# A two-layer graph network: routed experts in blocks of two sizes, and the key/value work of layer 1 in finer steps with its variances on ScalarE

## The chip, the core and the metric

The kernel runs on one core of a Trainium2 chip. A core has a matrix engine (TensorE; in the profile PE for its matmuls and PEld for its weight loads), a vector engine (VectorE, DVE), an engine for activation functions (ScalarE, ACT), a general engine that here mostly issues indirect transfers (GpSimd, POOL), an engine that issues plain transfers (SyncE, SP), and 16 DMA engines. Every engine works through its own queue in order, and the engines wait for each other by semaphores. The metric is the device time of one execution in microseconds (us), as the median of several.

## What is computed

The network has 3125 nodes with 256 features and 50000 edges sorted by target. Two layers are applied, each adding a message-passing branch, an attention-like branch and then a mixture of experts to the node features x, with layer norms before them. All arithmetic is float32. The parts that the change touches, in short:

```python
# layer 0, experts: 8 of them, every node goes to its best two
shared = gelu(x @ W1s + b1s) @ W2s + b2s
topw, topi = top_k(softmax(x @ Wr), 2)
routed = sum over the two of  weight_e * (gelu(x @ W1p[e] + b1p[e]) @ W2p[e] + b2p[e])
x = x + shared + routed                      # W1p[e] 256x1024, W2p[e] 1024x256

# layer 1, message passing: 4 heads, softmax over the edges into a node
messages = h_fwd[src] * direction[:, 0:1] + h_rev[src] * direction[:, 1:2]   # 64 wide
scores = leaky_relu(messages . attn[head], 0.2)
out[node, head] = sum of messages * exp(score) / sum of exp(score)

# layer 1, mixing: 8 heads of 64, linear in q
k = (k - mean(k)) / sqrt(var(k) + eps);  v = (v - mean(v)) / sqrt(var(v) + eps)
dots = sum over nodes of k^T v;  out = (q @ dots) / n @ Wout + bout
```

## The kernel before

Nodes are held in 25 tiles of 128. The stages run one after another: layer 0's messages and mixing, its shared and then its routed experts, layer 1's edge loop with the mixing beside it, and layer 1's experts. Two of them matter here.

**Routed experts (`layer0_ffn`).** Each (node, expert) pair gets a slot. The slots of one expert are filled up to a multiple of `BLK` = 256, so that every block of 256 slots belongs to one expert; there are `NBLK` = 32 blocks and 8192 slots whatever the routing gives. The generator `routes()` computes the slot numbers with small VectorE instructions and writes each node's row to its two slots with 50 indirect scatters from GpSimd. It is run in steps: `next(steps)` is called between the matmuls of the shared expert, twice per hidden chunk and per output tile, and after the routes the same chain of steps ranks a second sort's keys (`sort_by_high`), which layer 1's experts need.

For a block, `block_in` reads its expert's number, its rows (264 KB) and the expert's W1 (1 MB) and biases with SyncE; `block_second` loads W2 (1 MB). W1 and W2 have two buffers each. `block_turn` transposes the rows on TensorE (L1132) and works out gates and target rows with nine small VectorE instructions. `block_hidden` does 8 x 2 matmuls with W1 as the stationary operand and the block's 256 slots as the moving one (L1163), with a gelu on ScalarE after each pair (L1165); `block_out` does 8 matmuls per 128 slots with the 256 output columns moving (L1175), scales on VectorE (L1178, tile yo, four buffers) and scatters 128 rows with GpSimd. A float32 matmul shows as two passes in the profile. The order on TensorE is hidden(b), transposes(b+1), out(b-1). Nine steps of the chain follow each block. Once the ranks are done, `next(columns)` issues one of 256 scatters of the second sort (tile sorted) beside each gelu, seven or eight a block. These stages are ordered by the framework's scheduler.

**Edge loop (`layer1_mix`).** 391 columns of 128 edges are taken in 50 groups (`SPANS`: one of 4, then 8 each). GpSimd gathers 136 numbers for each edge, one indirect transfer per column (L71), into four group buffers. TensorE, VectorE and ScalarE are scheduled by hand here (`manual_schedule`): each works in the order of the program text. In round i that is:

- `messages(i)`: L1652 to L1662 on VectorE, ending with the maximum of the scores; TensorE transposes that (L1664);
- `weigh(i-1)`: exponents times messages (L1702, L1703, 2048 elements);
- `maximum(i)`: the running maximum (L1671 to L1673), spread over the partitions by TensorE (L1677);
- `products(i-1)`: 8 matmuls of 260 columns (L1709);
- `add(i-2)`: the block sums (VectorE L1717 and L1718, ScalarE copies L1719 and L1721);
- `ones_of(i)`: the one-hot matrix (L1695);
- `exponents(i)`: ScalarE copies the maximum out of PSUM (L1682, tile top_b), VectorE subtracts it (L1683), ScalarE takes the exponents (L1685, L1687);
- in three rounds of four until round 34, then in every one, one step of the generator `galerkin`, the mixing branch.

A step of `galerkin` handles two node tiles: for the tile before, VectorE reduces the squares to 16 variances (L1797), ScalarE takes the square root (L1801), VectorE inverts and scales (L1803, L1804) and TensorE adds to the dots (L1807); for the tile itself TensorE makes keys and values (two times four matmul passes, L276), ScalarE copies them out (L1817) and squares 1024 elements at once (L1819). After the 25 tiles come the weights' product and the final matmuls and adds (L1823 to L1864).

Of the kernel before, what the change touches and what calls it, by code (L numbers as in the profile page):

```python
# [9 lines left out]
F32 = mybir.dt.float32  # L10
# [4 lines left out]
OP = mybir.AluOpType  # L15
# [20 lines left out]
NBLK = 2 * N // BLK + 8  # L36
SLOTS = NBLK * BLK

# [92 lines left out]
class Kernel:  # L131
# [787 lines left out]
    def layer0_ffn(self, arrive, far, sorting):  # L919
# [3 lines left out]
        with ExitStack() as c:  # L923
# [83 lines left out]
            def routes():  # L1007
# [21 lines left out]
                for e in range(NE):  # L1029
                    nc.vector.tensor_tensor_scan(run[:, e, :], cnt[:, e, :], zero, 0.0, OP.add, OP.add)  # L1030
                nbi = big.tile([P, NE], I32, name="nbi")
                nb = big.tile([P, NE], F32, name="nb")
                yield
                nc.vector.tensor_scalar(nb, run[:, :, NT - 1], float(BLK - 1), None, op0=OP.add)
                yield
                nc.vector.tensor_copy(nbi, nb)
                yield
                nc.vector.tensor_scalar(nbi, nbi, BLK.bit_length() - 1, None, op0=OP.logical_shift_right)
                yield
                nc.vector.tensor_copy(nb, nbi)  # L1040
                end = big.tile([P, NE], F32, name="end")
                yield
                nc.vector.tensor_tensor_scan(end, nb, zero[:, :NE], 0.0, OP.add, OP.add)
                first = big.tile([P, NE], F32, name="first")
                yield
                nc.vector.tensor_sub(first, end, nb)


                nc.vector.tensor_sub(run, run, cnt)
                yield  # L1050
                nc.vector.scalar_tensor_tensor(run, first[:, :, None].to_broadcast([P, NE, NT]), float(BLK), run,
                                               op0=OP.mult, op1=OP.add)
                val = big.tile([P, NT, NE], F32, name="val")
                yield
                nc.vector.scalar_tensor_tensor(val, pre, 1.0, run.rearrange("p e t -> p t e"),
                                               op0=OP.add, op1=OP.add)
                yield
# [8 lines left out]
                for i in range(2):  # L1066
# [15 lines left out]
                nc.gpsimd.iota(which, pattern=[[1, NBLK], [0, NE]], base=0, channel_multiplier=0,  # L1082
                               allow_small_or_imprecise_dtypes=True)
                yield
                nc.vector.tensor_tensor(which, which, first[:1, None, :].to_broadcast([1, NBLK, NE]), OP.is_ge)  # L1085
# [23 lines left out]

            def block_in(b):  # L1110
                e = nc.sync.value_load(exi[0:1, b:b + 1], min_val=0, max_val=NE - 1)
# [4 lines left out]
                nc.sync.dma_start(r, self.slots[b * BLK:(b + 1) * BLK, :].rearrange("(i p) w -> p i w", p=128))  # L1116
# [10 lines left out]
            def block_turn(b, b2, r):  # L1127
                xs = hp.tile([128, 2, BLK], F32, name="xs")
                pt = self.ps_a([128, 2, SB, 128])
                for k in range(2):  # L1130
                    for i in range(SB):
                        nc.tensor.transpose(pt[:, k, i, :], r[:, i, k * 128:(k + 1) * 128], self.ident)  # L1132
                nc.vector.tensor_copy(xs, pt.rearrange("p k i b -> p k (i b)"))  # L1133

                own = hp.tile([128, SB, 4], F32, name="own", bufs=3)
                at, mine = own[:, :, 3], own[:, :, 0:2]
                nc.vector.tensor_scalar(at, base, float(b * BLK), None, op0=OP.add)
                nc.vector.tensor_tensor(mine, r[:, :, D + 2:D + 4],
                                        at[:, :, None].to_broadcast([128, SB, 2]), OP.is_equal)
                gt = hp.tile([128, SB, 2], F32, name="gt")  # L1140
# [3 lines left out]
                to = hp.tile([128, SB, 2], F32, name="to")  # L1144
# [6 lines left out]
                nc.vector.scalar_tensor_tensor(toi, at, 2.0 * NP, own[:, :, 0], op0=OP.add, op1=OP.add)  # L1151
                bg = hp.tile([128, SB, D], F32, name="bg", bufs=3)
                for i in range(SB):
                    nc.scalar.activation(bg[:, i, :], b2, AF.Copy, scale=own[:, i, 2:3])
                return xs, own, toi, bg

            def block_hidden(b, w1, b1, xs):
                few = FC - 1 - b % 2
                h = hp.tile([128, FC, BLK], F32, name="h")
                for f in range(FC):  # L1160
                    ph = self.ps_b([128, BLK])
                    for k in range(2):
                        nc.tensor.matmul(ph, w1[:, k, f * 128:(f + 1) * 128], xs[:, k, :],  # L1163
                                         start=(k == 0), stop=(k == 1))
                    ins = nc.scalar.activation(h[:, f, :], ph, AF.Gelu, bias=b1[:, f:f + 1])  # L1165
                    if ranked and f <= few:
# [4 lines left out]
            def block_out(w2, h, own, to, bg):  # L1171
                for i in range(SB):
# [12 lines left out]
            ins = {b: block_in(b) for b in range(2)}  # L1185
            w2 = {b: block_second(ins[b][0]) for b in range(2)}
            turned = block_turn(0, *ins[0][3:])
            output(*pending)
            todo = None
            for b in range(NBLK):  # L1190
                e, w1, b1, _, _ = ins.pop(b)
                xs, *rest = turned
                h = block_hidden(b, w1, b1, xs)
                if b + 2 < NBLK:
                    ins[b + 2] = block_in(b + 2)
                if b + 1 < NBLK:
                    turned = block_turn(b + 1, *ins[b + 1][3:])
                if todo is not None:
                    block_out(w2.pop(b - 1), *todo)
                    if b + 1 < NBLK:  # L1200
                        w2[b + 1] = block_second(ins[b + 1][0])
                for _ in range(9):
                    ranked = next(steps, sorted_) is sorted_
                todo = h, *rest
            block_out(w2.pop(NBLK - 1), *todo)
# [1434 lines left out]
```

## Time and profile before

| | us |
|---|---|
| three runs | 2496.76, 2501.61, 2501.92; median 2501.61 |
| the profiled execution | 2496.96, span 2495.2 |
| routed experts, first hidden matmul to last output matmul | 941.5 to 1398.1 |
| edge loop, first to last gather | 1463.7 to 1978.1 |
| busy over the span | PE 2052.0, DVE 1465.5, ACT 829.8, POOL 1565.4 |

The profile is taken from one execution on the chip. A group line gives the source line, engine, operation, tiles written and read, shape and count, then the busy time, the mean nanoseconds of one instruction, and the idle time of its engine just before it with what ended that. A timeline line gives the start, the length, engine, line, operation, tiles and shapes; a bracket gives the idle time before it and what released it. A line of a stretch gives each engine's busy time in it, the granted TensorE clock as a share, the busy share of the DMA engines and GB/s.

### The profile page before, as it was taken

How to read it: one execution, taken by the hardware profiler on the slowest of the kernel's cores; microseconds unless marked ns; L12 is line 12 of the kernel's file. 1: busy time of each engine (PE TensorE's matmuls, PEld its weight loads, DVE VectorE, ACT ScalarE, POOL GpSimd, SP SyncE). 2: the span in 40 equal slices, each digit the busy share in tenths (PEclk: the TensorE clock that was granted, in tenths of full speed). 3: DMA queues.
4: the chain of work that ended last, by engine and by line, in shares of the span. 5: the costliest groups of instructions: out<-in, count | busy, mean ns of one | idle time of the engine just before them, and what ended most of it. 6: DMA issues, size and time to landing. Idle time of an engine off the chain costs nothing.

```text
span 2495.2 us, 27313 instructions
## 1 busy us (share of the span) xinstructions
PE 2052.0 (82%) x8239; PEld 1450.5 (58%) x8239; DVE 1465.5 (59%) x3870; ACT 829.8 (33%) x1804; POOL 1565.4 (63%) x1931
## 2 busy tenths in 40 slices
PE   1666799899879989999999647777778779999955
PEld 0433355445555678888888535545556566667644
DVE  6888858986724793221212448888887872223346
ACT  1453144564412113333333324444430042222314
POOL 5888888885000816766666247777776427777743
PEclk9986799999959999999999869999989859999977
DMA  8612539113000225666666332222222112113242
GB/s 269 217 63 102 219 134 324 68 62 111 7 34 5 102 77 164 201 193 200 198 191 187 116 99 55 56 55 56 55 62 46 38 27 38 28 21 80 57 126 78
DMA packets 191721, 263.31 MB, mean 106 GB/s; under 512 B 57234, under 2 KB 152071, under 8 KB 191563
## 3 DMA queue, kind: packets, MB, share of 16 engines
q1 hardware_dynamic: 137551, 211.02, 25.5%
q0 software_dynamic: 48864, 45.64, 8.8%
q10 hardware_dynamic: 5148, 4.80, 0.7%
q8 instruction: 67, 1.10, 0.2%
q14 instruction: 91, 0.75, 0.1%
HBM read 180.80 MB, written 80.55 MB: 105 GB/s over the span
## 4 chain that ended last, share of the span: by engine, by line
PE 59%; DVE 23%; ACT 5%; DMA 4%; POOL 4%; issue 4%; ACTq 0%; DVEq 0%; SPq 0%; POOLq 0%
PE pb L1163 9%; PE pc L1175 8%; PE pb L594 7%; PE fpy L1958 7%; PE fph L1942 7%; DVE v L1703 3%; PE pc L594 3%; PE pw L1709 2%; PE pb L967 2%; PE pc L980 2%; POOL adj L78 2%; PE pb L638 2%; POOL g L71 1%; PE pc L1439 1%; DVE msg L1653 1%
## 5 line engine op out<-in xcount | busy, mean ns | idle before, releaser
L71 POOL DMA_INDIRECT g<-tab,t_src x391 | 378.3, 968 | 197.4 <-issue 153.2
L78 POOL DMA_INDIRECT adj<-ch_sum,ch_place x391 | 415.3, 1062 | 91.0 <-issue 56.5
L78 POOL DMA_INDIRECT sorted<-src,pos x256 | 245.1, 958 | 141.6 <-DVE pos L1462 62.1
L71 POOL DMA_INDIRECT G<-tabg,g_src x256 | 257.9, 1008 | 78.0 <-DMA G<-tabg,g_src 35.7
L1163 PE MATMUL pb<-xs,w 128*128 128x256 f32 x1024 | 226.4, 379 | 0.8 <-ACT h L1165 0.8
L1175 PE MATMUL pc<-w,h 128*128 128x256 f32 x1024 | 226.1, 379 | 0.0
L1709 PE MATMUL pw<-v,hot 128*128 128x260 f32 x782 | 219.5, 442 | 0.0
L1163 PEld LDWEIGHTS pb<-xs,w 128*128 128x128 f32 x1024 | 194.4, 190 | 27.8 <-ACT h L1165 1.0
L594 PE MATMUL pb<-adj,sup 128*128 128x448 f32 (+1 forms) x484 | 196.5, 551 | 14.3 <-DVE r_tot L1309 13.6
L1175 PEld LDWEIGHTS pc<-w,h 128*128 128x128 f32 x1024 | 192.2, 190 | 24.9
L1165 ACT ACTIVATE h<-pb,b 128x256 f32<-128x256 f32 x256 | 121.2, 473 | 253.6 <-issue 168.1
L1709 PEld LDWEIGHTS pw<-v,hot 128*128 128x128 f32 x782 | 169.1, 222 | 31.3
L1958 PE MATMUL fpy<-fw,fh 128*128 128x256 f32 (+1 forms) x800 | 177.7, 379 | 0.0
L1942 PE MATMUL fph<-xT,fw 128*128 128x512 f32 (+2 forms) x448 | 175.2, 545 | 0.0
L1958 PEld LDWEIGHTS fpy<-fw,fh 128*128 128x128 f32 (+1 forms) x800 | 149.6, 187 | 31.8 <-issue 8.2
L78 POOL DMA_INDIRECT slots<-rows,abi x50 | 54.5, 1090 | 164.6 <-DVE which L1085 154.6
L1421 ACT ACTIVATE s_z<-s_y,s_val 128x128 f16<-128x128 f16 x256 | 112.4, 486 | 121.0 <-issue 108.2
L594 PEld LDWEIGHTS pb<-adj,sup 128*128 128x128 f32 x484 | 90.3, 194 | 91.6 <-issue 85.5
L1133 DVE COPY xs<-pa 128x512 f32<-128x512 f32 x32 | 22.1, 691 | 206.6 <-PE pa L1132 206.6
L1944 ACT ACTIVATE fh<-fph,cols 128x512 f32<-128x512 f32 (+2 forms) x112 | 70.3, 632 | 216.2 <-PE fph L1942 216.2
L1942 PEld LDWEIGHTS fph<-xT,fw 128*128 128x128 f32 x448 | 85.7, 192 | 76.7 <-issue 55.8
L1178 DVE SCALAR_TENSOR_TENSOR yo<-pc,own,bg 128x256 f32<-128x256 f32 x64 | 31.0, 484 | 147.0 <-PE pc L1175 147.0
(575 smaller groups left out, 3820.9 us busy)
## 6 DMA issues: line engine op xcount, KB each, us to landing
adj<-zero SPq DMA_DIRECT2D x25, 1600.0 KB
w<-in_L_ffn_W1p_dram SPq DMA_DIRECT2D x32, 1024.0 KB
w<-in_L_ffn_W2p_dram SPq DMA_DIRECT2D x32, 1024.0 KB
adj<-adj SPq DMA_DIRECT2D x24, 896.0 KB
adj<-adj SPq DMA_DIRECT2D x24, 704.0 KB
slots<-empty SPq DMA_DIRECT2D x1, 8448.0 KB
srow<-slots SPq DMA_DIRECT2D x32, 264.0 KB
adj<-ch_sum,ch_place POOLq DMA_INDIRECT x391
```

The lines of the kernel that those rows point to most:

```text
L71: return nc.gpsimd.indirect_dma_start(out=out, out_offset=None, in_=table, in_offset=bass.IndirectOffsetOnAxis(ap=idx, axis=0))
L78: return nc.gpsimd.indirect_dma_start(out=table, out_offset=bass.IndirectOffsetOnAxis(ap=idx, axis=0), in_=rows, in_offset=None, **kw)
L594: nc.tensor.matmul(pm[:, :w], sup[:, b, k * 128:(k + 1) * 128], mats[b, h][:, c0 - PARTS[h][0]:c0 - PARTS[h][0] + w], start=(b == b0), sto ...
L1163: nc.tensor.matmul(ph, w1[:, k, f * 128:(f + 1) * 128], xs[:, k, :], start=(k == 0), stop=(k == 1))
L1165: ins = nc.scalar.activation(h[:, f, :], ph, AF.Gelu, bias=b1[:, f:f + 1])
L1175: nc.tensor.matmul(py, h[:, f, i * 128:(i + 1) * 128], w2[:, f, :], start=(f == 0), stop=(f == FC - 1))
L1421: nc.scalar.activation(z[:, i, k, :], y, AF.Relu, bias=val[:, k, s], scale=val[:, 2 + k, s])
L1703: self.latest = nc.vector.tensor_mul(v[:, :n, :, :HD], o[:, :n, None, :HD].to_broadcast([128, n, 4, HD]), weight[:, :n, :, None].to_broadc ...
L1709: nc.tensor.matmul(pw.rearrange("p h c -> p (h c)"), hot[:, k, :], v[:, k, :, :].rearrange("p h c -> p (h c)"), start=(k == 0), stop=(k == ...
L1942: nc.tensor.matmul(ph[:, :m], w1[:, k, f * 128:(f + 1) * 128], xT[:, k, t0 * P:t0 * P + m], start=(k == 0), stop=(k == 1))
L1944: note(nc.scalar.activation(hs[:, f, :m], ph[:, :m], AF.Gelu, bias=self.col("L1_ffn_b1", ei * FC + f)), m / 512.0)
L1958: nc.tensor.matmul(py[:p], hs[:, f, i * P:i * P + p], w2[:, f, :], start=(f == 0), stop=(f == FC - 1))
```

## The change

Layer 0: 17 blocks of 256 slots are taken by whole 256s of each expert, in order, as far as 17 reach; what is left of each expert goes into 22 blocks of 128. That is 39 blocks and 7168 slots. The list `TURNS` mixes the two sizes evenly. `routes()` gets the instructions for the second kind of slot and six more steps. A block of 128 has half of the rows, transposes, hidden columns, output matmuls and result scatters, and the same weights. Five steps of the chain follow such a block in place of nine, and four or five columns are issued beside its gelus in place of eight.

Layer 1: the two multiplies of the messages become one. `galerkin` is paced by `advance`, which is called twice a round, before `add` and after `exponents`, and hands out 62 steps evenly over the first 46 rounds. A tile's work takes two steps: first the square root for the tile before, the matmuls, the copies and the squares; then the inverse, the scaling and the dots. The variances are made by ScalarE, as 16 squares of 64 elements that each leave their sum, in place of one square of 1024 and VectorE's reduction.

```diff
-NBLK = 2 * N // BLK + 8
-SLOTS = NBLK * BLK
+WHOLE = (2 * N - 8 * (BLK - 1) + BLK - 1) // BLK
+PART = 128
+PARTED = (2 * N - WHOLE * BLK + 8 * (PART - 1)) // PART
+NBLK = WHOLE + PARTED
+SLOTS = WHOLE * BLK + PARTED * PART
+TURNS = sorted(range(NBLK), key=lambda b: (2 * b + 1) / (2 * WHOLE) if b < WHOLE
+               else (2 * (b - WHOLE) + 2) / (2 * PARTED))
...
+                end = blocks("end", total, 0, BLK)
...
+                nc.vector.tensor_scalar(end, end, float(WHOLE), None, op0=OP.min)
...
+                part = blocks("part", total, PART - 1, PART)
...
+                nc.vector.tensor_tensor(beyond, val, split[:, None, :].to_broadcast([P, NT, NE]), OP.is_gt)
+                yield
+                nc.vector.tensor_mul(beyond, beyond, move[:, None, :].to_broadcast([P, NT, NE]))
...
+            def slot(b):
+                return b * BLK if b < WHOLE else WHOLE * BLK + (b - WHOLE) * PART
+            def lots(b):
+                return SB if b < WHOLE else PART // 128
...
-                        nc.tensor.matmul(ph, w1[:, k, f * 128:(f + 1) * 128], xs[:, k, :],
+                        nc.tensor.matmul(ph[:, :m], w1[:, k, f * 128:(f + 1) * 128], xs[:, k, :m],
                                          start=(k == 0), stop=(k == 1))
-                    ins = nc.scalar.activation(h[:, f, :], ph, AF.Gelu, bias=b1[:, f:f + 1])
-                    if ranked and f <= few:
+                    ins = nc.scalar.activation(h[:, f, :m], ph[:, :m], AF.Gelu, bias=b1[:, f:f + 1])
+                    if ranked and (b < WHOLE or f % 2 == 1 or (f == 0 and b % 2)):
...
-            for b in range(NBLK):
+            for i, b in enumerate(T):
...
-                for _ in range(9):
+                for _ in range(9 if b < WHOLE else 5):
                     ranked = next(steps, sorted_) is sorted_
...
-                nc.vector.tensor_mul(o[:, :n, :], g[:, :n, :W], sides[:, :n, 0:1].to_broadcast([128, n, W]))
-                nc.vector.tensor_mul(g[:, :n, W:], g[:, :n, W:], sides[:, :n, 1:2].to_broadcast([128, n, W]))
-                nc.vector.tensor_add(o[:, :n, :], o[:, :n, :], g[:, :n, W:])
+                both = g[:, :n, :].rearrange("p j (i w) -> p j i w", i=2)
+                nc.vector.tensor_mul(both, both, sides[:, :n, :, None].to_broadcast([128, n, 2, W]))
+                nc.vector.tensor_add(o[:, :n, :], g[:, :n, :W], g[:, :n, W:])
...
+                done, every = 0, 2 * NT + 12
+                def advance(half):
+                    nonlocal done
+                    while done * 2 * (S - 4) < half * every:
+                        next(todo, None)
+                        done += 1
...
                         summed[i - 1] = products(SPANS[i - 1][1], exps[i - 1][2], msg[i - 1][1])
+                    advance(2 * i + 1)
                     if 0 <= i - 2 < S:
                         add(i - 2, *exps[i - 2][:2], summed[i - 2])
...
                         exps[i] = exponents(n, s, pb)
-                    if i % 4 != 3 or i > 34:
-                        next(todo, None)
+                    advance(2 * i + 2)
...
         for t in range(NT + 1):
             if t > 0:
-                kv, sq = kvs.pop(t - 1)
-                var = wk.tile([P, 16], F32, name="kv_var")
-                nc.vector.tensor_reduce(var, sq, AX.X, OP.add)
-                nc.vector.tensor_scalar(var, var, 1.0 / 64, LN_EPS, op0=OP.mult, op1=OP.add)
+                kv, var = kvs.pop(t - 1)
+                nc.vector.tensor_scalar(var, var, LN_EPS, None, op0=OP.add)
                 both = wk.tile([P, 8], F32, name="kv_both")
                 nc.vector.tensor_mul(both, var[:, 0:8], var[:, 8:16])
                 nc.scalar.activation(both, both, AF.Sqrt)
+            if t < NT:
+                nxt = wk.tile([P, 16, 64], F32, name="kv")
+                for i in range(2):
+                    pk = ps_a.tile([P, 512], F32, name="ln_pt")
+                    self.token_matmul(pk, xT, t, wkv[:, :, 512 * i:512 * i + 512])
+                    nc.scalar.copy(nxt[:, 8 * i:8 * i + 8, :].rearrange("p a b -> p (a b)"), pk)
+                sq = wk.tile([P, 64], F32, name="kv_sq", bufs=1)
+                var = wk.tile([P, 16], F32, name="kv_var")
+                for h in range(16):
+                    nc.scalar.activation(sq, nxt[:, h, :], AF.Square, scale=0.125, accum_out=var[:, h:h + 1])
+                kvs[t] = nxt, var
+            yield
+            if t > 0:
                 inverse = both if scales is None else scales
                 nc.vector.reciprocal(inverse, both)
...
-            if t < NT:
-                kv = wk.tile([P, 16, 64], F32, name="kv")
...
-                sq = wk.tile([P, 16, 64], F32, name="kv_sq", bufs=1)
-                nc.scalar.activation(sq, kv, AF.Square)
-                kvs[t] = kv, sq
-            yield
+                yield
```

## The prediction

> **What bounds the kernel now.** I read the page first (busy shares, costliest groups), then a table of stretches with each engine's busy time, then the timeline of one edge group, engine by engine, and the waits of VectorE and GpSimd. The change touches two stages and each has its own limit, so the 82% of PE over the span says little.
>
> The routed experts run from 941.5 to 1398.1 us. One stretch of that stage, and one of the edge loop:
>
> ```profile
> core 0: us, PE busy (x) PEld busy (x) DVE busy (x) ACT busy (x) POOL busy (x), PEclk, DMA share, GB/s
> 1123.00:1185.00 62.00, 62.00 (x297) 54.55 (x296) 11.78 (x48) 21.57 (x46) 40.18 (x43) 1.00 0.65 201
> 1622.00:1684.00 62.00, 46.19 (x182) 30.42 (x183) 55.40 (x111) 27.54 (x56) 47.08 (x49) 0.97 0.25 56
> ```
>
> The reader is to see PE busy 62.00 of 62.00 us at full clock in the experts: nothing but fewer matmul columns shortens that stage. In the edge loop DVE is busy 89% (55.40 us); POOL shows 47.08 us, but each of its 49 gathers is followed by an idle 0.30 us that nothing releases, so 49 x 1.25 = 61 us and POOL is as full as DVE.
>
> The costliest groups of the page price both:
>
> ```profile
> L71 POOL DMA_INDIRECT g<-tab,t_src x391 | 378.3, 968 | 197.4 <-issue 153.2
> L1163 PE MATMUL pb<-xs,w 128*128 128x256 f32 x1024 | 226.4, 379 | 0.8 <-ACT h L1165 0.8
> L1175 PE MATMUL pc<-w,h 128*128 128x256 f32 x1024 | 226.1, 379 | 0.0
> ```
>
> A pass over 256 columns costs 226.4/1024 = 0.221 us. A block has 64 of them and four transposes: its W1 load is issued every 14.25 us (1099.63, 1113.88), and 32 blocks make 456.
>
> Then the order inside one edge group, on the three engines that keep the written order:
>
> ```profile
> 1641.01 3.77 PE L1709 MATMUL pw<-v,hot 128*128 128x260 f32 x16
> ...
> 1648.94 5.46 PE L1709 MATMUL pw<-v,hot 128*128 128x260 f32 x16
> ...
> 1655.13 3.60 PE L276 MATMUL ln_pt<-wkv,xT 128*128 128x512 f32 x8
> ...
> 1658.77 0.58 ACT L1817 COPY kv<-ln_pt 128x512 f32<-128x512 f32 x1 [1.13 <-PE ln_pt L276]
> ...
> 1659.38 1.06 ACT L1819 ACTIVATE kv_sq<-kv 128x1024 f32<-128x1024 f32 x1
> ...
> 1659.87 0.41 DVE L1717 TENSOR_TENSOR acc<-acc,grown 64x260 f32<-64x260 f32 x1
> ...
> 1661.16 0.17 ACT L1682 COPY top_b<-psm 128x8 f32<-128x8 f32 x1
> ...
> 1661.79 0.18 DVE L1683 TENSOR_TENSOR score<-score,top_b 128x32 f32<-128x32 f32 x1
> ```
>
> ScalarE's order is: kv copies, kv square, copies for acc, copy of top_b, exponents. DVE subtracts top_b (L1683) 1.9 us after it has the group's maximum (1659.87 to 1661.79), and in this group top_b came 0.5 us before it was needed. So ScalarE already arrives just in time, with one 1.06 us square in its queue.
>
> **Experts.** Before: 32 blocks of 256. After: 17 of 256 and 22 of 128, 7168 slots for 8192. Passes over 128 columns are in the trace: eight dots matmuls take 1.05 us (L1807 at 1654.24), the first 0.28, so 0.110 us each, weight loads included; half of 0.221. Output matmuls are per 128 rows as before. A half block is thus 7.12 us: 17 x 14.25 + 22 x 7.12 = 399, which is 57 less.
>
> What must stay hidden. Weights: each block still loads 2 MB; the stage's DMA share is 0.62, 8.9 us of engine time per block; a half block keeps about 8.2 (half the rows and results), and a 256 and a 128 block together need 17.1 us of their 21.4. Two halves in a row want 16.4 in 14.2; with a 256 before them the two buffers hold this (25.3 of 28.5). GpSimd: 256 sorted scatters and 56 result scatters (64 before) at 0.96 + 0.30 = 1.26 us are 394 us of 399; it starts only when the ranks are there (945.2), the scatters left over by the loop are already run first today (30 sorted ones before the first result scatter, at 983), and the results then wait in its queue with four yo buffers behind them. I bound that at 0 (it keeps up as today) to 25 us (yo stalls PE once per backlog), and take 7, near today's, where PE never waited for yo. DVE and ScalarE work per block is under half of its time. Routing: six more steps and some 14 more small DVE instructions of 0.16 to 0.5 us delay the slot scatters by about 5 us; the first block's rows were issued at 887.4 and first used at 923.8, so this costs nothing, or 5 if that slack is used up. The fill of the slots is 1 MB shorter, 0 to -3 us; I take 0. Experts: -50 (-57 to -25).
>
> **Edge groups, what leaves DVE.** Per token tile the reduction (1.21) goes and the add shrinks (0.33 to about 0.17); two message multiplies of 544 elements (0.72 and 0.71) become one of 1088: from 544 at 0.72 and 2048 at 2.29 that is 1.29, 0.1 less per group. In all 25 x 1.37 + 5 = 39 us of DVE work. If DVE were the limit, that would be the gain, up to where 391 gathers x 1.25 = 489 us bind (they take 514 now, 1463.7 to 1978.1).
>
> **Edge groups, what enters the path.** 62 steps are handed out over 46 groups, two chances a group, and a tile now takes two steps: A (square root, token matmuls, two copies, 16 squares with sums) and B (reciprocal, scaling, dots). Solving the pacing condition, A comes at every half number 3m and B at 3m+2. So three groups carry two tiles: in the first, A stands in the first place, before the group's own ScalarE work; in the second, B in the first place and A at the end; in the third, B at the end. Before, everything stood at the end.
>
> Price of 16 squares. The trace has this pair of instructions once, on 256 elements:
>
> ```profile
> 210.62 0.38 ACT L825 ACTIVATE sq<-pb 128x256 f32<-128x256 f32 x1 [0.79 <-PE pb L823]
> 210.90 0.19 ACT L825 ACTIVATION_READ_ACCUMULATOR sq<-pb 128x1 f32 x1
> 211.12 0.38 ACT L825 ACTIVATE sq<-pb 128x256 f32<-128x256 f32 x1
> ```
>
> A pair recurs after 0.50 us. ScalarE's rate (512 elements 0.687, 384 elements 0.580 in the expert rows) is 0.84 ns each, so 64 elements save 0.16: 0.34 us a head, 5.4 us a tile in place of 1.06. Bounds: 0.20 if the read runs under the next square, 0.37 if nothing overlaps. I take 0.34, the row's own.
>
> First group, from the moment its maximum is known: products start at 0.3 and take 3.77, the token matmuls follow at 3.9, the squares start 4.25 after these (1655.13 to 1659.38), at 8.1; 5.4 of squares, 0.6 for three small copies: top_b is there at 14.2. DVE needs it at 2.3 (1.9, and 0.4 for two kv instructions): it is held 11.8 us, and as it keeps its order, the next group's messages are held with it. From the subtraction to the next maximum it needs 5.9 (a group without kv takes 7.93, less 0.1, less 1.9). First group: 20.1.
>
> Second: PE stood idle, so the products cost 5.46 as at 1648.94; with dots (1.0) the tokens start at 6.5. The next group's transpose is queued behind them, so its maximum is known at 10.9, 2 us later than DVE could. The squares run from 10.8 to 16.2, top_b is there at 16.8 = 5.9 into the third group, whose DVE wants it at 1.9: 4 us more. After that 6.7 with the scaling. Second and third: 23.6.
>
> Three groups take 43.7 us, with 17.6 of waiting, where today four take 42.2 (1637.61 to 1679.8). Twelve such turns are 524 us for 36 groups that take 383.8 now (1490.0 to 1873.8): +140. With 0.20 a head, 39.2 a turn, +87; with 0.37 and a cold first product (1.7), 46.4, +173. The 39 us taken off DVE vanish in these waits. The last 13 groups carry the same closing matmuls and adds as before, in other places: 0. GpSimd's gathers wait for buffers instead of limiting.
>
> The Trainium skill, "ScalarE: Activation LUTs", section "What ACT_TABLE_LOAD costs", gives 186 ns plus 0.833 ns per element less 93 ns of overlap: an estimate of 0.15 us a head without any price for reading the sum, 37.5 us a turn, +66, and 2513 in all. Its section "Rules for kernel authors" wants adds and multiplies on VectorE and so speaks against this part. No run here shows 64-element squares.
>
> **Sum.** The profiled execution took 2496.96 us (span 2495.2), 4.7 below the median of 2501.61. 2497 - 50 + 140 = 2587.
>
> **Rivals.**
> 1. Faster: DVE isn't held, because the squares and copies pass ScalarE within today's half microsecond of margin. Then the gathers set the loop (489 for 514): 2497 - 50 - 25 = 2422. For it: ScalarE is busy 44% in this loop. Against: the order on ScalarE. The two parts cancel at +50, a turn of 36.1 us, which needs 0.10 us a head; ScalarE's smallest row in the loop (top_b) is 0.16.
> 2. Half blocks cost nearly a whole one: weight loads show 190 ns, and 32 x 0.19 = 6.1 for 3.5 us in the hidden half gives the 57 back (22 x 2.6); late weights would do the same. 2497 + 140 = 2637. Against: the dots row.
>
> **Chances.** The sum's mechanism 0.74, with a range of its own of 2497 + 87 - 57 = 2527 to 2497 + 173 - 25 = 2645; rival 1 0.12; rival 2 0.10; other mixtures 0.04. The range 2527 to 2645 takes in rival 2 and leaves rival 1 out. Under 0.2% (5 us) a change can't be told from none. Faster 0.13, same 0.02, slower 0.85.
>
> **What would show it.** Right: the experts' stretch about 50 us shorter with PE still full; half blocks 7.1 us apart; in the edge loop DVE's L1683 idle for ScalarE's top_b some 11 us in every third group and 4 in another; DVE's share down to about 60%; GpSimd waiting. Wrong: a loop of about 490 us with gathers end to end; W1 loads of half blocks 9 us or more apart; or pairs of square and read under 0.2 us.

## The result and the profile after

The changed kernel takes 2660.42 us (median of 4 runs, 2659.88 to 2661.17) against 2499.19 for the kernel before: a ratio of 1.0651, 95% interval 1.0624 to 1.0678. That is 163 us slower in the profiled executions (spans 2658.6 and 2495.2), where 90 had been forecast, and above the forecast's upper end of 2645. In some sets of runs every kernel is slower (the kernel before takes 2812 to 2838 us there in place of 2498 to 2500, and chip 4 has sets of both kinds, so the cause is not known), and what is compared below lies within one set or between sets of one kind, except where it says otherwise. Line numbers are now those of the changed kernel.

| profiled executions, us | before | after | difference | forecast |
|---|---|---|---|---|
| experts, first hidden matmul to end of last output matmul | 457.0 | 414.6 | -42.4 | -50 |
| start of that stage | 941.5 | 944.0 | +2.5 | 0 to 5 |
| edge loop, first gather to last maximum | 534.8 | 738.7 | +203.9 | +140 |
| of it: 36 groups from the second maximum on | 383.8 | 569.4 | +185.6 | +140 |
| of it: the last 12 intervals between maxima | 124.6 | 142.2 | +17.6 | 0 |

The costliest groups of the changed kernel's page already name the wait (the last two numbers are the engine's idle time before the group and how much of it ended with the named releaser):

```profile
L76 POOL DMA_INDIRECT g<-tab,t_src x391 | 374.2, 957 | 406.5 <-DVE own_bank L1747 225.5
...
L1728 DVE TENSOR_TENSOR score<-score,top_b 128x32 f32<-128x32 f32 (+2 forms) x50 | 9.3, 186 | 225.6 <-ACT top_b L1727 225.6
```

VectorE's subtraction of the maximum, 9.3 us of work, has 225.6 us of waiting for ScalarE's copy of it. GpSimd's gathers wait the same 225.5 us in turn. They do not wait for a buffer, as the prediction had it:

```profile
1639.88 0.72 DVE L1700 TENSOR_TENSOR msg<-g 128x544 f32<-128x544 f32 x1
...
1663.40 0.21 DVE L1707 TENSOR_REDUCE mx<-score 128x4 f32<-128x32 f32 x1
...
1663.88 0.94 POOL L76 DMA_INDIRECT g<-tab,t_src  x1 [12.84 <-DVE own_bank L1747]
```

The buffer that this gather fills was last read at 1640.60, a round earlier. In both kernels `request(2, self.latest)` puts the first gather of a group behind the maximum of the scores (L1707; the profile names L1747, which follows it at once), and this maximum comes late because VectorE was held. The stretches show both stages:

```profile
core 0: us, PE busy (x) PEld busy (x) DVE busy (x) ACT busy (x) POOL busy (x), PEclk, DMA share, GB/s
1080.00:1120.00 40.00, 40.00 (x224) 36.15 (x223) 10.46 (x48) 14.58 (x35) 30.24 (x32) 1.00 0.78 251
...
1452.00:2021.00 569.00, 328.48 (x1065) 226.22 (x1063) 296.57 (x595) 266.72 (x1100) 284.79 (x298) 0.74 0.17 37
```

In the experts TensorE is still full, with the DMA share up from 0.65 to 0.78. In the edge loop VectorE is busy 52% of the time (296.57 of 569 us) and no engine is near full. TensorE's granted clock is 0.74 there; in the same groups of the kernel before VectorE was busy 88% and the clock was 0.93:

```profile
1490.00:1874.00 384.00, 286.04 (x1092) 194.23 (x1092) 336.55 (x670) 159.45 (x330) 289.06 (x299) 0.93 0.25 56
```

The timeline of the first round of one turn, cut to the lines that matter:

```profile
1640.87 0.21 DVE L1707 TENSOR_REDUCE mx<-score 128x4 f32<-128x32 f32 x1
...
1644.04 0.35 PE L1722 MATMUL psm<-ident,top 4*128 4x4 f32 x2 [2.53 <-DVE top L1717]
...
1644.32 5.70 PE L1754 MATMUL pw<-v,hot 128*128 128x260 f32 x16
...
1649.85 3.60 PE L281 MATMUL ln_pt<-wkv,xT 128*128 128x512 f32 x8
...
1653.97 0.26 ACT L1862 ACTIVATE kv_sq<-kv 128x64 f32<-128x64 f32 x1
1654.13 0.19 ACT L1862 ACTIVATION_READ_ACCUMULATOR kv_sq<-kv 128x1 f32 x1
1654.35 0.26 ACT L1862 ACTIVATE kv_sq<-kv 128x64 f32<-128x64 f32 x1
...
1660.50 0.17 ACT L1727 COPY top_b<-psm 128x8 f32<-128x8 f32 x1
...
1660.69 0.19 DVE L1728 TENSOR_TENSOR score<-score,top_b 128x32 f32<-128x32 f32 x1 [14.42 <-ACT top_b L1727]
```

From the maximum at 1640.87 the chain runs through the products (5.70 us, after an idle 2.53 on TensorE, which had also stood 0.88 and 3.52 us shortly before; the granted clock over these 5.70 us is 0.65), the token matmuls, two copies and sixteen squares 0.38 us apart, and only then comes the copy of 0.17 us that VectorE stands 14.42 us for. The third round of a turn has a second such wait of 4.24 us. A turn takes 47.6 us (1593.4 to 1640.9 to 1688.6).

### The profile page after: what moved, and what is told of

The parts are those of the page before. It is cut to its first block, busy times and chain, and to the rows that moved or that the text cites. A ratio compares the mean times of both kernels' runs of the same rounds, so it can differ in the third digit from the quotient of the medians.

```text
span 2658.6 us, 28419 instructions
## 1 busy us (share of the span) xinstructions
PE 2061.2 (78%) x8319; PEld 1459.5 (55%) x8319; DVE 1436.5 (54%) x3877; ACT 945.4 (36%) x2627; POOL 1563.1 (59%) x1924
## 4 chain that ended last, share of the span: by engine, by line
PE 60%; DVE 18%; ACT 7%; POOL 6%; issue 4%; DMA 4%; ACTq 0%; DVEq 0%; SPq 0%; POOLq 0%
PE pb L1207 7%; PE pc L1219 7%; PE pb L599 7%; PE fph L1997 6%; PE fpy L2013 6%; PE pw L1754 6%; ACT kv_sq L1862 5%; POOL adj L83 3%; PE ln_pt L281 3%; DVE v L1748 3%; PE pb L972 2%; PE pc L599 2%; PE pc L985 2%; DVE g L1699 2%; PE pb L643 1%
## 5 line engine op out<-in xcount | busy, mean ns | idle before, releaser
L76 POOL DMA_INDIRECT g<-tab,t_src x391 | 374.2, 957 | 406.5 <-DVE own_bank L1747 225.5
L1754 PE MATMUL pw<-v,hot 128*128 128x260 f32 x782 | 256.6, 499 | 0.0
L1754 PEld LDWEIGHTS pw<-v,hot 128*128 128x128 f32 x782 | 195.3, 256 | 42.2
L1207 PE MATMUL pb<-xs,w 128*128 128x128 f32 (+1 forms) x1248 | 205.7, 324 | 9.4 <-issue 8.8
L1207 PEld LDWEIGHTS pb<-xs,w 128*128 128x128 f32 x1248 | 188.3, 195 | 25.5 <-issue 9.5
L1219 PE MATMUL pc<-w,h 128*128 128x256 f32 x896 | 199.7, 380 | 0.0
L1209 ACT ACTIVATE h<-pb,b 128x128 f32<-128x128 f32 (+1 forms) x312 | 128.9, 413 | 180.2 <-PE pb L1207 106.9
L1219 PEld LDWEIGHTS pc<-w,h 128*128 128x128 f32 x896 | 167.5, 190 | 21.0
L1728 DVE TENSOR_TENSOR score<-score,top_b 128x32 f32<-128x32 f32 (+2 forms) x50 | 9.3, 186 | 225.6 <-ACT top_b L1727 225.6
L1709 PE MATMUL psm<-ident,mx 128*4 128x128 f32 x50 | 16.3, 325 | 134.2 <-DVE mx L1707 134.2
```

Of the source, the lines that this page charges most:

```text
L76: return nc.gpsimd.indirect_dma_start(out=out, out_offset=None, in_=table, in_offset=bass.IndirectOffsetOnAxis(ap=idx, axis=0))
L1207: nc.tensor.matmul(ph[:, :m], w1[:, k, f * 128:(f + 1) * 128], xs[:, k, :m], start=(k == 0), stop=(k == 1))
L1209: ins = nc.scalar.activation(h[:, f, :m], ph[:, :m], AF.Gelu, bias=b1[:, f:f + 1])
L1219: nc.tensor.matmul(py, h[:, f, i * 128:(i + 1) * 128], w2[:, f, :], start=(f == 0), stop=(f == FC - 1))
L1754: nc.tensor.matmul(pw.rearrange("p h c -> p (h c)"), hot[:, k, :], v[:, k, :, :].rearrange("p h c -> p (h c)"), start=(k == 0), stop=(k == ...
```

## The experiments

Ratios are to the kernel before in the same set of runs. Many kernels first fell in a slower set and were run again (label with _b); the expectations call such a set a slower chip. Two of the repeats, `merged_only_b` and `double_squares_b`, fell in a slower set too. A "turn" is three rounds of the loop, which carry two tiles. My theory: layer 1 loses because ScalarE's queue has the copies and squares of a tile ahead of top_b; two things can make that long, the squares and the place of the step. Rivals: the squares' amount of work on ScalarE, or the even pacing by itself.

**One part at a time** (`blocks_alone`, `groups_alone`): the changed layer 0 with the old layer 1, and the reverse.

> The changed layer 0 with layer 1 as before. If the two parts add, as the traces say: the experts' stage is 42 us shorter and starts 2.5 later, so 40 us less than before, some 2459, and an edge loop of 535 us from the first gather to the last maximum, as before. Rival, that the blocks of two sizes leave something behind that slows the edge loop (late gathers, a cold clock): the loop is longer than 535 by more than 5 us.

> The changed layer 1 with layer 0 as before. If the parts add: +204 us on before, some 2703, with 24 waits of VectorE for top_b that sum to 216 us in the 36 groups with key/value work. Rival, that part of the 204 comes from layer 0: under +190.

Both fell in a slower set. There `groups_alone` is 1.0587 (1.0531 to 1.0643) of before, and the 36 groups take 628.1 us against 476.1 with the old layer 1, 152 more. In all it loses 164 us, less than the 190 below which part of the loss was to come from layer 0; a slower set cannot settle that, and `blocks_deep` below does (with the changed layer 0 the loop is as before): the loss belongs to layer 1. `blocks_alone` is 1.0024 (0.9988 to 1.0061): no gain. The experts show it: 514.2 us with blocks of two sizes, 483.7 with the old blocks in `groups_alone` of the same set (whose profiled execution was the fastest of five, by 27 us). Three of the longest waits of `blocks_alone` over its whole span (total, times, longest), and then one of them in the timeline:

```profile
ACT kv L1862 <- remote: 140.5, 10, 14.9
...
ACT h L1209 <- remote: 116.8, 20, 16.8
DVE yo L1222 <- remote: 109.2, 20, 16.4
```

```profile
1837.90 3.60 PE L281 MATMUL ln_pt<-wkv,xT 128*128 128x512 f32 x8
...
1849.82 1.07 ACT L1862 COPY kv<-ln_pt 128x512 f32<-128x512 f32 x2 [14.87 <-remote]
```

These are stops of up to 23.1 us (on ScalarE's fh) whose releaser the profile calls "remote" only. All ten traces from slower sets have them, the ten others none. The five groups with most of this waiting all read a product of TensorE: here the token matmuls have ended at 1841.50 by the profile, and ScalarE's copy of them starts 8.3 us later. DMA packets of 2 KB and more take 159 ns in the median in both kinds of set. Why the products come late is open, so the question of one part alone was put again, as `blocks_deep`.

**The squares taken away, the place kept** (`one_square`):

```diff
-                sq = wk.tile([P, 64], F32, name="kv_sq", bufs=1)
-                var = wk.tile([P, 16], F32, name="kv_var")
-                for h in range(16):
-                    nc.scalar.activation(sq, nxt[:, h, :], AF.Square, scale=0.125, accum_out=var[:, h:h + 1])
-                kvs[t] = nxt, var
+                sq = wk.tile([P, 16, 64], F32, name="kv_sq", bufs=1)
+                nc.scalar.activation(sq, nxt, AF.Square)
+                kvs[t] = nxt, sq
```

and the reduction on VectorE as before.

> The changed kernel, but with one square of 1024 elements and the reduction on VectorE again; the places of the steps stay. Squares theory (what holds VectorE is the length of ScalarE's queue ahead of top_b): a tile's squares fall from 6.1 to 1.06, so the wait of the first group falls from 14.4 to 9.4 us and the one of the third from 4.2 to about 0, and VectorE gets 1.4 us a tile: a turn of three groups goes from 47.6 to about 41.1, 78 us less, some 2582. Place theory (token matmuls and copies ahead of the group's own work cost nearly all): only 27 us less, some 2633. If the squares were the whole cause: the loop of before, some 2465.

> The same kernel as one_square, since the chip of that run had the kernel before at 2812 us. Squares theory: on a chip where the kernel before takes 2500 us, 78 us less than the changed kernel's 2660, some 2582. Place theory: some 2633. Squares as the whole cause: some 2465. The shares seen on the slower chip (a loop 90 us longer than the loop before, where the full change had 176) speak for about half: 2560 to 2585.

In the slower set 1.0317 (1.0248 to 1.0387); in the other 2537.94 us, 1.0156 (1.0139 to 1.0173): 122 us under the changed kernel, more than the 78 of the squares theory and than the range of 2560 to 2585. VectorE's waits there, from 1452 to 2100 us:

```profile
DVE score L1728 <- ACT top_b L1727: 101.0, 14, 9.3
```

The wait of the third round is gone, and that of the first is 7.6 to 8.6 us in the turns, where the squares theory had 0 and 9.4. A turn takes 37.6 us rather than 41.1; the likely reason, not tested, is that the reduction's 1.4 us a tile that I had added lies in time in which VectorE waits anyway. The loop is still 616.6 us: the squares are not the whole cause.

**The place moved, the squares kept** (`spread_late`):

```diff
                         summed[i - 1] = products(SPANS[i - 1][1], exps[i - 1][2], msg[i - 1][1])
-                    advance(2 * i + 1)
...
                         exps[i] = exponents(n, s, pb)
+                    advance(2 * i + 1)
                     advance(2 * i + 2)
```

> The changed kernel with both calls of advance at the end of the round, after the exponents; 16 squares on ScalarE as changed. Place theory: the wait of 14.4 us becomes one of the kind that the third group has (4.2 us), a turn of three groups goes from 47.6 to about 37.4, 122 us less, some 2538. Rival (the squares' length alone counts, wherever they stand): no change, 2660.

> The same kernel as spread_late, for the same reason. Place theory: some 2538. Squares' length alone: 2660. By the share seen on the slower chip (67 of 176 us left): some 2535.

1.0294 (1.0243 to 1.0345) in the slower set, 2530.42 us and 1.0121 (1.0103 to 1.0139) in the other: 130 us under the changed kernel, 122 forecast. A turn is 37.4 us (14.1 + 8.1 + 15.2) as worked out; from the 26th round on, where two steps fall into other rounds, about 34. What is left:

```profile
DVE score L1728 <- ACT top_b L1727: 96.1, 26, 4.7
```

The long wait of 14.4 is gone; every tile now holds VectorE for up to 4.7 us, as only the third round's did.

**Both** (`one_square_late`):

> The changed kernel with both edits: one square and VectorE's reduction, and both calls of advance at the end of the round. What is left of the change in layer 1 is the even pacing, the split of a tile's work and the merged multiply. Theory (squares and place together make the loss): the edge loop is back at 525 to 545 us from first gather to last maximum (535 before), the time at about 2460. Rival (the even pacing, two tiles in three groups, costs by itself): over 2480.

2449.53 us, 0.9805 (0.9784 to 0.9825): faster than before. The loop takes 529.4 us, and the 36 groups 360.8 where before's took 383.8. So the even pacing does not cost. The 23 us between them are not all gain: TensorE makes 26 matmuls fewer in these groups (x1066 here, x1092 before) and 24 more in the last 12 intervals, which take 142.5 us for 124.6. Over the whole loop 5.4 us are left.

```profile
1445.00:1806.00 361.00, 282.89 (x1066) 196.91 (x1064) 325.38 (x623) 155.66 (x325) 273.56 (x288) 0.92 0.22 56
```

288 gathers of 0.95 us with 0.30 between them are 360 us: here GpSimd is the limit, as rival 1 of the prediction had it for the case that VectorE isn't held. With the two edits singly (447.6 and 440.3 us in the 36 groups) and neither (569.4), each alone takes off 122 and 129 us, both 209: they overlap by 42.

**The squares' place in the queue** (`squares_lagged`): all steps at the end of the round, and a tile's 16 squares one tile later, ahead of the next tile's copies.

```diff
-            if t > 0:
-                kv, var = kvs.pop(t - 1)
+            if t > 1:
+                kv, var = squared.pop(t - 2)
...
+            if 0 < t <= NT:
+                kv1 = kvs.pop(t - 1)
...
+                for h in range(16):
+                    nc.scalar.activation(sq, kv1[:, h, :], AF.Square, scale=0.125, accum_out=var1[:, h:h + 1])
+                squared[t - 1] = kv1, var1
             if t < NT:
-                nxt = wk.tile([P, 16, 64], F32, name="kv")
+                nxt = wk.tile([P, 16, 64], F32, name="kv", bufs=3)
```

> The changed kernel with all steps at the end of the round, as in spread_late, and ScalarE's 16 squares for a tile made one tile later, ahead of the next tile's copies: the same 6.1 us of squares a tile, but they start when the exponents are out and wait for no matmul of their own group. Queue theory (the loss is what stands ahead of top_b while VectorE waits, not ScalarE's total work): ScalarE has some 25 us of work in a turn of three groups that lasts 30, VectorE is hardly held, and the 36 groups with key/value work take 361 to 375 us, like one_square_late's 360.8; the whole 2450 to 2465. Work theory (16 pairs of 0.38 us are too much for ScalarE wherever they stand): the 36 groups take 420 us or more, as in spread_late (440.3), the whole over 2505.

> The same kernel as squares_lagged. Queue theory: 36 groups in 361 to 375 us, the whole 2450 to 2465. Work theory: 36 groups in 420 us or more, the whole over 2505. The run on the slower chip (no waits of VectorE for top_b among its longest) speaks for the queue theory.

1.0115 (1.0043 to 1.0187) in a slower set; 2448.34 us, 0.9796 (0.9779 to 0.9812) in the other. The stretch of the 36 groups, to be read against the changed kernel's (1452.00:2021.00 above), and a round of the timeline:

```profile
1447.00:1809.00 362.00, 286.30 (x1057) 196.89 (x1056) 296.93 (x596) 260.95 (x1100) 274.74 (x287) 0.89 0.22 56
...
1606.56 0.24 ACT L1858 ACTIVATE kv_sq<-kv 128x64 f32<-128x64 f32 x1
...
1611.50 3.77 PE L1754 MATMUL pw<-v,hot 128*128 128x260 f32 x16
...
1612.51 1.05 ACT L1865 COPY kv<-ln_pt 128x512 f32<-128x512 f32 x2
...
1614.06 0.17 ACT L1727 COPY top_b<-psm 128x8 f32<-128x8 f32 x1
...
1614.26 0.19 DVE L1728 TENSOR_TENSOR score<-score,top_b 128x32 f32<-128x32 f32 x1 [1.03 <-ACT top_b L1727]
```

VectorE and ScalarE do the same work in both (296.93 and 296.57; 260.95 and 266.72 us), in 362 and in 569 us. The squares run from 1606.56 while TensorE makes the next tile, the copies follow without a wait, and VectorE waits 1.03 us. Against `spread_late_b`, whose steps have the same places (62 of them, 63 with the lag), the lag takes the 36 groups from 440.3 to 362.3 us, 1.5 above `one_square_late`. So it is not the amount of the squares: 6.1 us a tile cost next to nothing where ScalarE would wait anyway, and hold VectorE where they stand between a fresh matmul and top_b.

**The squares doubled** (`double_squares`: each made twice, same result).

> The changed kernel with each of the 16 squares made twice (same result): 12.2 us of pairs a tile in place of 6.1. Queue theory: the wait of the first group goes from 14.4 to 20.5 us and that of the third from 4.2 to 10.3, a turn of three groups from 47.6 to about 59.8, 146 us more over twelve turns, some 2806. Place theory (token matmuls and copies, not the squares): under 2700.

> The same kernel as double_squares. Queue theory: waits of 20.5 and 10.3 us in a turn of 59.8, some 2806. Place theory: under 2700.

Both runs fell in slower sets: 1.1255 (1.1147 to 1.1364) and 1.1154 (1.1074 to 1.1234). The stated times can't be met there; the waits can be read. In the second run the longest is 21.4 us (20.5 forecast), and the 36 groups take 784.2 us against 628.1 of `groups_alone` in another slower set, 13.0 a turn for the 12.2 forecast. VectorE's waits for top_b sum to 420.2 us against 274.9 there: 6.05 us more for each of 24 tiles, whose squares take 6.1 more.

**The scatter that frees toi** (`blocks_deep`): the changed layer 0 with the old layer 1 and

```diff
-                toi = hp.tile([128, SB], I32, name="toi", bufs=4)
+                toi = hp.tile([128, SB], I32, name="toi", bufs=10)
...
-                    yo = hp.tile([128, D], F32, name="yo", bufs=4)
+                    yo = hp.tile([128, D], F32, name="yo", bufs=5)
```

> The changed layer 0 with ten buffers for toi in place of four and five for yo in place of four, layer 1 as before. In the changed kernel TensorE stands idle 8.8 us at block 6 and then runs 3.0 us longer at half clock, because VectorE waits 19.0 us for a result scatter that frees toi. Theory: that goes, the experts' stage falls from 414.6 to about 403 us and the whole to 52 under the kernel before, some 2448. Rival (the four or five yo buffers bind next, at the same scatters): the stage stays within 4 us of 414.6, the whole at about 2460. The edge loop stays at 535 if blocks of two sizes leave nothing behind.

2445.57 us, 0.9798 (0.9774 to 0.9822). In the changed kernel's timeline the target rows of a later block wait for an old result scatter, and the transposed rows for TensorE are queued on VectorE behind them:

```profile
1002.57 0.96 POOL L83 DMA_INDIRECT y<-yo,toi  x1 [0.31 <-issue]
...
1009.56 0.16 DVE L1195 SCALAR_TENSOR_TENSOR toi<-own 128x2 int32<-128x2 f32 x1 [19.04 <-DMA y<-yo,toi]
...
1010.59 6.76 PE L1207 MATMUL pb<-xs,w 128*128 128x128 f32 x32 [8.11 <-issue]
```

TensorE stands 8.11 us and then takes 6.76 for passes that take 3.73 elsewhere. In `blocks_deep`:

```profile
998.55 0.16 DVE L1195 SCALAR_TENSOR_TENSOR toi<-own 128x1 int32<-128x1 f32 x1
...
1000.07 3.73 PE L1207 MATMUL pb<-xs,w 128*128 128x128 f32 x32
```

The stage takes 403.2 us (403 forecast), the edge loop 533.1 (534.8 before): blocks of two sizes leave nothing behind for the loop, and VectorE's yo, which now waits up to 11.1 us, doesn't stop TensorE. The two buffer counts were raised together; that toi alone is enough was not tested.

**Pacing or multiply** (`merged_only`: `blocks_deep` with the one message multiply).

> blocks_deep with the message multiply merged into one instruction, otherwise layer 1 as before. one_square_late's 36 groups took 360.8 us where before's took 383.8 and blocks_deep's 384.0. Pacing theory (even steps make that gain): the merged multiply is worth its 0.1 us a group, the 36 groups take about 380, the whole about 2441. Multiply theory: the groups fall by 15 to 23 us, the whole to 2422 to 2430.

> The same kernel as merged_only. Pacing theory: 36 groups in about 380 us, the whole about 2441, 0.1 us a group under blocks_deep's 2445.6. Multiply theory: 36 groups in 361 to 369, the whole 2422 to 2430.

Both in slower sets (1.0017, 0.9977 to 1.0056; 0.9977, 0.9932 to 1.0023). The 36 groups take 475.2 us in `merged_only_b` and 476.1 in `blocks_alone` of another such set: 0.9 us for the multiply where 3.6 were expected. But such sets can't decide between the theories. In the set of `merged_only` its 36 groups take 462.9 us, and those of `even_late_closing` below, with the even pacing, 461.9: the pacing shows no gain there either. What part of the 23 us of `one_square_late` is the multiply, the pacing or moved work stays open.

**The closing rounds** (`even_late_closing`, `early_closing`, `lagged_early`). All have the deeper buffers and all steps at the end of the round; once the steps with tiles are done, one closing step a round:

```diff
-                    while done * 2 * (S - 4) < half * every:
+                    while done < every and done * 2 * (S - 12) < half * every:
...
-                    advance(2 * i + 1)
-                    advance(2 * i + 2)
+                    if done < every:
+                        advance(2 * i + 2)
+                    else:
+                        next(todo, None)
```

`early_closing` has S - 15, `lagged_early` S - 17 with the lagged squares; the other two have one square.

> Changed layer 0 with ten toi and five yo buffers; layer 1 with one square and VectorE's reduction, steps at the end of the round, the 51 steps with tiles over the first 38 rounds and then one closing step a round as before. If the terms add: one_square_late's 2449.5, less 11.4 for the scatters (blocks_deep), less 17 for the closing rounds (142.5 to about 125 us from the 37th maximum on, as before): about 2421. Rival for the closing term (it is not the handing out of two steps in one round that costs there): no gain from it, about 2438.

> The same kernel as even_late_closing. If the terms add: about 2421, with the rounds from the 37th maximum on at about 125 us in place of 142.5. Rival: 142 there, the whole about 2438.

> even_late_closing with the tile steps over the first 35 rounds in place of 38, so that the closing steps, one a round, end three rounds before the last group. If what was missing is their place: the 13 or so us by which the last eight rounds outlast the gathers shrink by three rounds of about 3 us, the loop from first gather to last maximum falls from 522 to about 512, the whole to about 2425. Rival (VectorE has no room for more tile steps a round: 1.46 a round are too many): the 36 groups rise from 360.7 by 10 us or more, and the whole stays at 2434 or above.

> squares_lagged with ten toi and five yo buffers, the tile steps over the first 33 rounds and then one closing step a round. If ScalarE can make 1.55 steps a round (about 9.5 us of its work in a round of 10): the groups stay bound by the gathers at 10.0 us a round, the loop falls to about 508, the whole to about 2421, level with early_closing or a few us under it. Rival (ScalarE's squares now reach into the next group's top_b): waits of VectorE for top_b over 40 us, the whole over 2440.

In a slower set `even_late_closing` is 1.0045 (1.0001 to 1.0089); in the others the three take 2434.11 us (0.9738, 0.9718 to 0.9758), 2432.99 (0.9738, 0.9724 to 0.9751) and 2440.61 (0.9767, 0.9753 to 0.9781). There all beat both kernels; the best is 2.6% faster than before. But the loop of `even_late_closing` fell by 7.5 us (529.4 to 521.9), not by 17, and putting the closing steps three rounds sooner changed nothing (522.6, for about 512 forecast). My account of the closing rounds as two steps in one round explains less than half of their price; the rest is open. In `lagged_early` the waits for top_b are back at 25.6 us (15.0 in `squares_lagged_b`), its 36 groups take 375.2 us and the loop 528.5, for about 508 forecast: at 52 steps in 33 rounds, 1.58 a round, ScalarE's squares reach into the next group's top_b again.

## Why the prediction was wrong

The direction and the mechanism on VectorE and ScalarE were right: the experts gain, VectorE is held at L1728 by ScalarE's top_b in the first and third round of every turn, the time taken off VectorE (39 us forecast, 444.8 - 409.0 = 35.8 measured in the loop) vanishes in the waits, and the gathers wait instead of limiting, though for the maximum and not for buffers. What failed is the term of the edge loop, +140, which measured +203.9: a turn was put at 43.7 and took 47.6, which is 47 of the 64 us that were missed, and the last groups were put at nothing and cost 17.6.

- **Experts, -50.** Measured -42.4, and +2.5 at the start. A whole and a half block take 21.5 us (21.37 forecast), a second half in a row 7.46 (7.12): 402.8 in place of 399, which is far from rival 2's 2.6 us a half block. The backlog of scatters, taken at 7, cost 8.1 idle and 3.0 at a lower clock; the tile that runs out is toi, allotted a block earlier than yo.
- **A head's square, 0.34.** 0.38 measured (0.26 for the square, 0.19 for reading the sum, 0.07 of overlap), just beyond the upper bound of 0.37: 0.7 us a tile. That bound was worked out wrongly: 0.38 less 0.16 for the square and 0.19 for the reading, with nothing overlapping, are 0.41, which would have held it. The Trainium skill's page "ScalarE: Activation LUTs", section "What ACT_TABLE_LOAD costs", gave an estimate of 0.15 without a price for the reading, and the trace shows that the reading makes half of the pitch. Its section "Rules for kernel authors", which wants adds and multiplies on VectorE, pointed the right way, yet `squares_lagged_b` (362.3 us) against `one_square_late` (360.8) shows that the squares cost next to no time in the right place, and gain none either.
- **First round, 20.1.** Measured 22.5. I had the products start warm (3.77) though TensorE stands idle 2.53 us ahead of them; they took 5.70. The second round was priced that way, the first only in the upper bound (1.7). With the squares' 0.7 that is the wait of 14.4 in place of 11.8.
- **Second and third, 23.6.** 9.1 and 16.0 measured; the third's wait is the forecast 4 us (4.24), and 2.68 for the transposed maximum behind the token matmuls where 2 was forecast. A turn is 47.6, beyond its bounds of 39.2 to 46.4 too.
- **The last 13 groups, 0.** The other 17.6 us. I costed them at nothing because the work is the same; no bound of the range held anything for them. It isn't quite the same: TensorE makes 412 matmuls there for 394, and in some rounds two closing steps fall together; `even_late_closing_b`, with one a round, got back 7.5 us, and the rest of the price is open. Without them the time would have been 2643, inside the range, but by luck: the range also allowed the experts a gain of only 25.
- **The rivals.** Rival 1's condition (ScalarE inside its margin) did not hold, but its limit is the true one: with the place mended and the squares either taken away or lagged, the 36 groups run near the gathers' 360 us (360.8 and 362.3); with the place alone they take 440.3. The forecast had the even pacing as neutral, which holds within 5.4 us over the loop of `one_square_late`. Rival 2 is ruled out by the half blocks at 7.46 us.

## What to carry to other kernels

On an engine that keeps its written order, price a moved instruction by what stands behind it: the same 16 squares cost next to nothing when their inputs were a round old, and were 6.1 of a wait of 14.4 us when they stood between a fresh matmul and a copy that another engine needed. A step added ahead of a matmul group that follows an idle TensorE must be priced with the slow products, not the warm ones, and work that "only changes places" needs an upper bound that is not zero. When a change has two parts, run each part alone: here the blocks were worth 40 us (53 with deeper buffers), outweighed by what the waits cost. And when a stretch gets shorter, count the work in it: part of the 23 us of the 36 groups came back as 17.9 in the groups after them.

## What was not expected of the hardware

TensorE's granted clock fell with the stalls: 0.92 in the 36 groups of `one_square_late`, 0.74 in the changed kernel's. A group's products take 3.77 us in 21 of the 36 groups of the one and in 12 of the other's, and 5.2 to 6.8 in nearly all others; a stall of another engine comes back as slower matmuls. And a gain need not carry over from one set of runs to another: where the "remote" stops show up, 5.5 to 14 us each in the mean for the three groups shown, the half blocks took longer than the whole ones (514.2 against 483.7 us), and `even_late_closing`, 2.6% faster than before elsewhere, is 0.4% slower.
